# The first group of layer 2: B's parts between the softplus steps, six units from B's rows, the third softplus behind the first scan

## The chip, the core and the metric

The kernel runs on one core of a Trainium2 chip. The core has five engines, each with its own queue of instructions, which it works off in order: TensorE (PE, matrix products; its weight loads are shown as PEld), VectorE (DVE), ScalarE (ACT), GpSimd (POOL) and SyncE (SP), which here only issues transfers. Sixteen DMA engines move data between DRAM and the on-chip memories: SBUF, which every engine reads, and PSUM, which TensorE writes. The engines wait for one another by semaphores only. The metric is the device time of one launch in microseconds; the text gives all times in microseconds (us).

## What is computed

The reference passes an image of 64 x 64 positions and 96 channels through two layers. A layer normalises in groups, projects to 192 inner channels (and 192 more for a gate), runs a 3 x 3 convolution and a silu, and then four selective scans over the 4096 positions, in four orders. The scan is the costly part:

```
x_dbl = u @ x_proj;  dt = softplus(x_dbl[:6] @ dt_proj + bias);  B, C = x_dbl[6:22], x_dbl[22:38]
h[t] = h[t-1] * exp(dt[t] * A) + (dt[t] * u[t]) * B[t]      # for 192 channels x 16 states
y[t] = sum over the 16 states of h[t] * C[t];  y += u * D
```

The four y are put back in order and summed, normalised over channels, multiplied by the gate and projected to 96 channels, and the layer's input is added. The change is in layer 2's scans.

## The kernel before

Channels and states lie on the 128 partitions, positions along the free axis. Layer 2's scans (`scans`) run over 16 **groups** (one order and one chunk of 1024 positions each, `GROUPS`), and a group over 24 **units** (`units`): 3 blocks T of channels times 8 pairs m of states, in the order T = 0, 0, 1, 1, 2, 2 with even and odd m in turn. `PER` is 24. A unit j is made in these steps, one function each:

- `stage_a` (ACT): a = exp(dt * A), 128 x 1024.
- b, the input of the recurrence, in PSUM, in one of two ways. **By rows**: `stage_B` (PE) spreads two rows of B over the partitions with two bfloat16 products, and `stage_b` (DVE) multiplies them by du = dt * u. **By tokens**: `product` (ACT) multiplies du, transposed so that positions lie on the partitions (`duT`), by a column of B transposed (`BT`), sixteen such products for three units of odd m, and `stage_t` (PE) transposes eight pieces of the result `bT` back into PSUM; DVE has no part in it. Before, even units go by rows, odd ones by tokens.
- `stage_s` (DVE): the scan h = a * h + b. `stage_k` (ACT): the last column kept for the next chunk. `stage_c` (POOL): hc = h * C. `stage_r` (PE): sums over states; a block's first unit also brings in y.

What a group needs ahead of its units is its **prelude**: `project` (PE: pj = the rows of B, C and dt's input, in two halves h of 512 positions), `projected` (ACT: the copy xd), `first_part`, `less_part` and `next_part` (ACT and PE in turn: B split into three bfloat16 parts, B3, by subtracting what was rounded), `rows` (SP: C to DRAM), `tokens_B` and `tokens_B_out` (PE, ACT: BT), `delta` (softplus in three parts per block: `begin` on PE gives pd; `by_scalar`, four ACT instructions; `by_vector`, four DVE instructions, whose third is the last to read pd and writes sp = dt, whose fourth writes su = dt * u), `spread` (SP four transfers of sp to dt; for group 0 POOL issues four of su to du), `tokens_du` and `tokens_du_out` (PE, ACT: duT).

The order of all work is written out by hand: a queue of an engine holds what the program emits, in that order. The main loop runs over j and emits in iteration j, among others, `fetch_c` (SP: rows of C broadcast into cb), b's PE step of unit j+1, `stage_a(j+2)`, `stage_b(j)`, `stage_r(j-3)`, `stage_s(j)`, `stage_k(j-1)`, `stage_c(j-1)`, and then every step of the preludes whose slot is below j+1. Group k's slots count from the start of group k-1, so that group 1's prelude (`at[1]`) is emitted in group 0's units: `project` of half 0 in iteration 0, its copies and parts and the subtracting products in iterations 1 and 2, `project` of half 1 in iteration 2, and so on.

Group 0 has no group ahead of it. Its prelude is `first`, emitted whole before the loop: the six `start_y` of the layer's head on POOL (`later`, y = u * D), the projection, the ACT table load, the three softplus, then the split of B, the transposes of du and the sixteen products of the first three odd units (four on ACT, eight on DVE, four on POOL).

PSUM is shared by tags: a tile may be written only when the last reader of the tile before it under the same tag is done. Group 1's projections, its pd and its `tokens_B` all use tag "v", one after another; in `first`, pd of block 2 has "v", that of blocks 0 and 1 has "y2" and "b1". The products' b lie in "b0" and "b1". Tiles of a and h have three buffers each, so `stage_a(j)` waits for the scan of unit j-3, and the scan of unit j for `stage_c(j-3)`.

Of the kernel before, what the change touches and what calls it, by code (L numbers as in the profile page):

```python
# [9 lines left out]
F32 = mybir.dt.float32  # L10
# [14 lines left out]
TC = 1024  # L25
# [19 lines left out]
def two_ss2d_layers(  # L45
# [41 lines left out]
    def load_exp_ln():  # L87
        table("natural_log_exp_and_others")
# [17 lines left out]
    for h in range(2):  # L106
        t = const.tile([128, 128], F32, name=f"wide{h}")
# [49 lines left out]
    with tc.tile_pool(name="ld", bufs=8) as ld, tc.tile_pool(  # L157
        name="ldp", bufs=4, space=PSUM
# [81 lines left out]
    def decays(am):  # L240

        for a, e, D in am:
            for h, half in enumerate(HALF):
                tc.keep_in_program_order(
                    nc.scalar.activation(a[half, 0, 0:D], e[half, 0:D, :, h:NS:2], AF.Exp)
                )
            nc.vector.tensor_scalar_mul(a[:, 1, 0:D], a[:, 0, 0:D], -0.5)
            nc.vector.tensor_scalar_mul(a[:, 0, 0:D], a[:, 0, 0:D], -1.0)
        return [a for a, e, D in am]
# [15 lines left out]
    class Ordered:  # L265
# [7 lines left out]
    pe, act, dve, pool, sp = (  # L273
        Ordered(e) for e in (nc.tensor, nc.scalar, nc.vector, nc.gpsimd, nc.sync)
    )
# [516 lines left out]
    def scans(weights, pps, ready, later):  # L792
# [4 lines left out]
        xw, dwb, _ = weights  # L797
        class Ordered:
# [9 lines left out]
        pe, act, dve, pool, sp = (  # L808
            Ordered(e) for e in (nc.tensor, nc.scalar, nc.vector, nc.gpsimd, nc.sync)
        )  # L810
        with ExitStack() as sc:
# [42 lines left out]
            def prelude(k):  # L854
# [65 lines left out]
                def tokens_du(e):  # L920

                    ps = me["ps"] = me["tu", e] = spare(
                        f"tu{k}_{e}", "v" if k else ("y2", "v", "b0", "b1")[e]
                    )
                    for T in range(3):
                        pe.transpose(
                            ps[:, 128 * T : 128 * (T + 1)],
                            me["su", T][:, 128 * e : 128 * (e + 1)], ident,
                        )

                def tokens_du_out(e):
                    t = me["duT", e] = pre.tile(
                        [128, 2, 3, 64], F32, tag=f"duT{e}", name=f"duT{k}_{e}"
                    )
                    copy = act.copy if k or e < 2 else dve.tensor_copy
                    copy(t, me["tu", e][:, 0:384].rearrange("p (b h c) -> p h b c", h=2, c=64))


                def delta(T):
# [82 lines left out]

                steps = []
                if k == 0:
                    first(
                        project, projected, rows, delta, spread, tokens_B, tokens_B_out,
                        first_part, less_part, next_part, tokens_du, tokens_du_out,
                    )
                    return products(k)
                if (p, d) == (1, 0):  # L1030
                    steps += [(-17 + T, lambda T=T: turn(T)) for T in range(3)]

# [30 lines left out]
            def first(  # L1063
                project, projected, rows, delta, spread, tokens_B, tokens_B_out,
                first_part, less_part, next_part, tokens_du, tokens_du_out,
            ):
                parts = [delta(T) for T in range(3)]
                for start in later:
                    start()
                for h in range(2):  # L1070
                    project(h)
                for h in range(2):
                    projected(h)
                load_exp_ln()
                rows()
                for begin, by_scalar, by_vector in parts:
                    begin()
                tokens_B()
                for T, (begin, by_scalar, by_vector) in enumerate(parts):
                    by_scalar()  # L1080
                    if T == 1:
                        tokens_B_out()
                        am.extend(decays(weights[2]))
                    by_vector()
                    spread(T)
                    if T < 2:
                        fetch_c(0, T)
                stage_a(0)
                for h in range(2):
                    first_part(h)  # L1090
                for h in range(2):
                    less_part(h)
                for h in range(2):
                    next_part(0, h)
                for h in range(2):
                    less_part(h)
                for e in range(4):
                    tokens_du(e)
                for e in (0, 2, 1, 3):
                    tokens_du_out(e)  # L1100
                for h in range(2):
                    next_part(1, h)
                for e, engine in enumerate((act, dve, dve, pool)):
                    for h in range(2):
                        for n in range(2):
                            product(0, 0, e, h, n, engine)
                stage_B(0)
                stage_a(1)

            def products(k):  # L1110


                turns = (
                    (19, (4, 4, 4, 4)), (PER, (3, 1, 5, 1, 3, 3)), (PER + 6, (4, 2, 3, 1, 3, 3)),
                    (PER + 12, (2, 3, 3, 2, 3, 3)),
                )
                steps = []
                for i, (slot, counts) in enumerate(turns):
                    if (k, i) == (0, 0):
                        continue  # L1120
                    todo = [(e, h, n) for e in range(4) for h in range(2) for n in range(2)]
                    for s, count in enumerate(counts):
                        steps += [
                            (slot + s + 0.1, lambda i=i, at=at: product(k, i, *at))
                            for at in todo[:count]
                        ]
                        del todo[:count]
                return steps

            def product(k, i, e, h, n, engine=act):  # L1130


                me = state[k]
                if (h, n) == (0, 0):
                    me["bT", i, e] = mn.tile(
                        [128, 2, 3, 2, 64], F32, tag="bT", name=f"bT{k}_{i}{e}", bufs=7
                    )
                q = 2 * (2 * i + 1) + n
                (act.mul if engine is act else engine.tensor_scalar_mul)(
                    me["bT", i, e][:, h, :, n, :], me["duT", e][:, h],  # L1140
                    me["BT"][:, e + 4 * h, q : q + 1],
                )
# [55 lines left out]
            def fetch_c(k, m):  # L1198
                cb = state[k]["C", m] = mn.tile([128, TC], F32, tag="cb", name=f"cb{k}_{m}")
                for h, half in enumerate(HALF):  # L1200
                    q = 2 * m + h
                    sp.dma_start(
                        out=cb[half], in_=state[k]["C"][q : q + 1, :].to_broadcast(cb[half].shape)
                    )

            def stage_B(j):

                k, T, m = units[j]
                ps = live["b", j] = pps.tile([128, TC], F32, tag="b0", name=f"b{j}")
                for s in halves:  # L1210
                    pe.matmul(
                        ps[:, s], pick(GROUPS[k][1], m), state[k]["B3"][:, s], start=True, stop=True
                    )
# [14 lines left out]
            def stage_a(j):  # L1228
                k, T, m = units[j]
                p, d, c = GROUPS[k]  # L1230
                a = live["a", j] = mn.tile([128, TC], F32, tag="a", name=f"a{j}")
                act.activation(
                    a, state[k]["dt", T], AF.Exp, scale=am[p][:, 0, d, T, m : m + 1]
                )
# [60 lines left out]
            def unit(step, at):  # L1295
                if 0 <= at < N:
                    step(at)

            for j in range(N + LAG + 2):

                for ahead, odd in ((4, 0), (1, 1)):
                    k, i = divmod(j + ahead, PER)
                    if i % 6 == 0 and 0 <= k < len(GROUPS):
                        fetch_c(k, i // 3 + odd)
                unit(stage_B if j % 2 else stage_t, j + 1)
                while early and early[0][0] < j + 1:
                    early.pop(0)[1]()
                unit(stage_a, j + 2)
                if j % 2 == 0:
                    unit(stage_b, j)  # L1310
                unit(stage_r, j - LAG)
                unit(stage_s, j)
                unit(stage_k, j - 1)
                unit(stage_y, j - LAG - 1)
                unit(stage_c, j - 1)
                while steps and steps[0][0] < j + 1:
                    steps.pop(0)[2]()
# [594 lines left out]
```

## Time and profile before

| what | us |
|---|---|
| median of 3 runs (lowest, highest) | 1472.04 (1468.18, 1472.88) |
| the profiled execution, its own time | 1467.99 |
| its span | 1466.2 |
| busy in the span: DVE / ACT / POOL / PE | 1331.0 / 1222.5 / 1222.4 / 1195.6 |
| layer 2's last convolution product ends, its scans' first product starts (PE) | 245.5 |
| first scan of layer 2 starts (DVE) | 274.74 |

A timeline line gives the start (us from the span's start), the length, the engine, the instruction with output and inputs, how many of them are merged, and in brackets the engine's idle time before it with what seems to have ended it. A windows line gives a stretch, its length, the busy time and count of PE, PEld, DVE, ACT and POOL, then the share of TensorE's full clock that was granted (PEclk), the busy share of the DMA engines (which may pass 1 a little) and GB/s. All kernel work in `scans` carries one line number, L806, that of a helper, so tiles tell the steps apart: pj is `project`, tu `tokens_du`, b from B and selh `stage_B`, b from b and du `stage_b`, b from ident and bT `stage_t`, ys `stage_r`, sp, su and wl the softplus.

### The profile page before, as it was taken

The page shows a single profiled execution, that of the slowest core. Times are in us where ns is not written, and L with a number is a line of the kernel's source. Part 1 is how long each engine was busy: PE and PEld are TensorE (multiplying, and loading weights), DVE is VectorE, ACT ScalarE, POOL GpSimd, SP SyncE. Part 2 cuts the span into 40 slices and gives each one's busy share as a digit, 9 for nine tenths or more (in the row PEclk, how much of TensorE's full clock was granted, in tenths as well). Part 3 has the DMA queues.
Part 4 walks back from the last instruction along what each step waited for, and adds up shares of the span by engine and source line. Part 5 has one row for each costly group of instructions (what it writes and reads, how often), then busy time and mean ns, then how long its engine had stood idle before and what let it go on. Part 6 is the DMA issues. An engine that isn't in the chain of part 4 may idle for free.

```text
span 1466.2 us, 17295 instructions
## 1 busy us (share of the span) xinstructions
PE 1195.6 (82%) x5019; PEld 461.4 (31%) x5019; DVE 1331.0 (91%) x920; ACT 1222.5 (83%) x2517; POOL 1222.4 (83%) x684
## 2 busy tenths in 40 slices
PE   5865768688988797988898889788888888887887
PEld 2233223233333333333333333333333232322333
DVE  5958576689999999999999999999999999999996
ACT  4873557599899989999999999999898989897874
POOL 2735348588989898989898989898989898989895
PEclk8987879699999999999999999999999999999999
DMA  3251522526262626262626262626262626262635
GB/s 108 70 136 18 136 69 88 131 58 146 58 146 58 146 59 144 60 144 60 144 60 144 60 144 60 144 60 145 62 151 61 146 68 137 70 142 67 140 87 129
DMA packets 86261, 148.66 MB, mean 101 GB/s; under 512 B 34060, under 2 KB 37196, under 8 KB 86060
## 3 DMA queue, kind: packets, MB, share of 16 engines
q1 hardware_dynamic: 84188, 144.00, 41.0%
q0 software_dynamic: 864, 2.49, 0.7%
q10 hardware_dynamic: 1104, 0.98, 0.2%
q8 instruction: 40, 0.66, 0.2%
q14 instruction: 65, 0.53, 0.1%
HBM read 81.77 MB, written 12.17 MB: 64 GB/s over the span
## 4 chain that ended last, share of the span: by engine, by line
DVE 28%; issue 23%; POOL 10%; ACT 10%; PE 9%; DMA 7%; SPq 2%; DVEq 0%; POOLq 0%; ACTq 0%
DVE h L806 18%; DVE b L806 8%; POOL hc L806 7%; DMA cb<-C 4%; ACT a L806 3%; ACT bT L806 2%; PE ys L806 2%; SPq L806 2%; PE pj L806 1%; PE b L806 1%; POOL sp L806 1%; DMA xT<-xs 1%; DMA du<-su 1%; POOL ln L806 1%; PE cp L271 1%
## 5 line engine op out<-in xcount | busy, mean ns | idle before, releaser
L806 POOL TENSOR_TENSOR hc<-h,cb 128x1024 f32<-128x1024 f32 x384 | 902.3, 2368 | 91.4 <-DVE h L806 38.2
L806 DVE TENSOR_TENSOR_SCAN h<-a,carry,b 128x1024 f32<-128x1024 f32 x288 | 665.2, 2338 | 24.9 <-PE b L806 3.9
L806 ACT ACTIVATE a<-dt,am 128x1024 f32<-128x1024 f32 x384 | 438.1, 1141 | 63.3 <-DVE h L806 57.6
L806 PE MATMUL ys<-hc,fold 128*64 128x512 f32 x1536 | 429.5, 638 | 0.5 <-POOL hc L806 0.5
L806 ACT ACTIVATE bT<-duT,BT 128x192 f32<-128x192 f32 x1012 | 387.1, 445 | 3.4 <-PE b L806 1.3
L806 PE MATMUL b<-ident,bT 128*128 128x128 f32 x1536 | 220.0, 286 | 28.9 <-DVE h L806 21.0
L806 DVE TENSOR_TENSOR b<-b,du 128x1024 f32<-128x1024 f32 x192 | 232.0, 1208 | 4.9 <-PE b L806 4.9
L806 DVE TENSOR_TENSOR_SCAN h<-a,b 128x1024 f32<-128x1024 f32 x96 | 216.2, 2277 | 11.8 <-POOL hc L806 2.8
L806 PE MATMUL b<-B,selh 96*128 96x512 bf16 x384 | 116.2, 384 | 130.6 <-DVE h L806 129.7
L806 PEld LDWEIGHTS b<-ident,bT 128*128 128x128 f32 x1536 | 174.4, 145 | 151.3 <-DVE h L806 90.4
L806 PEld LDWEIGHTS ys<-hc,fold 128*64 128x64 f32 x1536 | 77.9, 138 | 141.7 <-issue 103.6
L806 PEld LDWEIGHTS <-selh 96*128 96x128 bf16 x384 | 25.8, 97 | 257.1 <-DVE h L806 201.0
L271 POOL TENSOR_TENSOR tap<-tap,tap 128x512 f32<-128x512 f32 x48 | 61.0, 1274 | 45.8 <-ACT tap L271 43.4
L806 PE MATMUL pj<-u,xw 64*124 64x512 f32 x192 | 91.5, 621 | 1.9 <-DVE w L806 1.2
L271 DVE SCALAR_TENSOR_TENSOR acc<-pad,v,acc 128x1052 f32<-128x1052 f32 (+1 forms) x64 | 75.3, 1182 | 2.1
L806 PE MATMUL ys<-y,ident 128*128 128x512 f32 (+1 forms) x120 | 59.6, 598 | 0.0
L806 ACT CAST B<-pj 96x512 bf16<-96x512 f32 (+2 forms) x96 | 54.9, 575 | 4.6 <-PE pj L806 4.5
L806 POOL TENSOR_TENSOR sp<-sp,ln 128x512 f32<-128x512 f32 x45 | 57.5, 1279 | 0.2
L806 POOL TENSOR_TENSOR ln<-ln,w 128x512 f32<-128x512 f32 x45 | 57.6, 1280 | 0.0
L806 POOL TENSOR_TENSOR su<-sp,u 128x512 f32<-128x512 f32 x45 | 57.4, 1276 | 0.0
L806 PE MATMUL pd<-xd,dwb 29*64 29x512 f32 x192 | 53.9, 634 | 0.0
L806 PEld LDWEIGHTS pj<-u,xw 64*124 64x124 f32 x192 | 33.1, 187 | 58.5 <-issue 44.1
(186 smaller groups left out, 1185.2 us busy)
## 6 DMA issues: line engine op xcount, KB each, us to landing
cb<-C SPq DMA_DIRECT2D x256, 256.0 KB
dt<-sp SPq DMA_DIRECT2D x192, 128.0 KB
du<-su SPq DMA_DIRECT2D x180, 128.0 KB
szd<-sz SPq DMA_DIRECT2D x24, 256.0 KB
szt<-szd SPq DMA_DIRECT2D x24, 256.0 KB
xT<-xs SPq DMA_DIRECT2D x8, 384.0 KB
xs<-xT SPq DMA_DIRECT2D x1, 1536.0 KB
xs<-xT SPq DMA_DIRECT2D x8, 192.0 KB
```

The source lines that it names most:

```text
L271: return lambda *args, **more: tc.keep_in_program_order(op(*args, **more))
L806: return lambda *args, **more: tc.keep_in_program_order(op(*args, **more))
```

## The change

In `first`, the ACT table load and `decays` (four small ACT exponentials, four DVE scalings) move ahead of the copies `projected`. The third softplus' `by_vector` and its `spread` leave `first` and become steps with slots `PER - 0.6` and `PER - 0.5` of group 0, that is -0.6 and -0.5 in the loop's count, emitted at the end of iteration 0, behind the first scan and ahead of group 1's first `project`. B's three parts are made between the softplus of the blocks, where before they came after all three. `tokens_du` and its copies move into iterations 1 and 2 (pieces 0 and 1, then 2 and 3), with all copies on ACT and PSUM tags "y2" and "y1"; within iteration 2 the order on PE is piece 2, group 1's `project` of half 1, piece 3. The sixteen products of units 1, 3 and 5 are dropped: units 0 to 5 all go by rows. The products of units 7, 9 and 11 are emitted at the end of iterations 2 to 5, four each. The last `start_y` on POOL moves to iteration 5.

```diff
 def tokens_du(e):
     ps = me["ps"] = me["tu", e] = spare(
-        f"tu{k}_{e}", "v" if k else ("y2", "v", "b0", "b1")[e]
+        f"tu{k}_{e}", "v" if k else ("y2", "y1")[e % 2]
     )
 ...
 def tokens_du_out(e):
 ...
-    copy = act.copy if k or e < 2 else dve.tensor_copy
-    copy(t, me["tu", e][:, 0:384].rearrange("p (b h c) -> p h b c", h=2, c=64))
+    act.copy(t, me["tu", e][:, 0:384].rearrange("p (b h c) -> p h b c", h=2, c=64))
 ...
 if k == 0:
-    first(
+    steps += first(
 ...
-    return products(k)
+    return steps + products(k)
 ...
 def first(...):
     parts = [delta(T) for T in range(3)]
-    for start in later:
+
+    def softplus(T):
+        parts[T][1]()
+        parts[T][2]()
+        spread(T)
+
+    for start in later[:-1]:
         start()
     for h in range(2):
         project(h)
+    load_exp_ln()
+    am.extend(decays(weights[2]))
     for h in range(2):
         projected(h)
-    load_exp_ln()
     rows()
     for begin, by_scalar, by_vector in parts:
         begin()
     tokens_B()
-    for T, (begin, by_scalar, by_vector) in enumerate(parts):
-        by_scalar()
-        if T == 1:
-            tokens_B_out()
-            am.extend(decays(weights[2]))
-        by_vector()
-        spread(T)
-        if T < 2:
-            fetch_c(0, T)
-    stage_a(0)
+    softplus(0)
+    fetch_c(0, 0)
     for h in range(2):
         first_part(h)
     for h in range(2):
         less_part(h)
+    tokens_B_out()
+    softplus(1)
+    fetch_c(0, 1)
     for h in range(2):
         next_part(0, h)
     for h in range(2):
         less_part(h)
-    for e in range(4):
-        tokens_du(e)
-    for e in (0, 2, 1, 3):
-        tokens_du_out(e)
     for h in range(2):
         next_part(1, h)
-    for e, engine in enumerate((act, dve, dve, pool)):
-        for h in range(2):
-            for n in range(2):
-                product(0, 0, e, h, n, engine)
     stage_B(0)
+    parts[2][1]()
+    stage_a(0)
     stage_a(1)
+    steps = [(PER - 0.6, parts[2][2]), (PER - 0.5, lambda: spread(2))]
+    for e in range(4):
+        o = PER + 1 + e // 2
+        steps += [
+            (o, lambda e=e: tokens_du(e)), (o + 0.1, lambda e=e: tokens_du_out(e)),
+        ]
+    return steps + [(PER + 5, later[-1])]
 ...
     if (k, i) == (0, 0):
         continue
+    if (k, i) == (0, 1):
+        slot, counts = PER + 2.3, (4, 4, 4, 4)
 ...
+def by_rows(j):
+    return j % 2 == 0 or j < 6
+
 def stage_B(j):
-    ps = live["b", j] = pps.tile([128, TC], F32, tag="b0", name=f"b{j}")
+    ps = live["b", j] = pps.tile([128, TC], F32, tag=f"b{j % 2}", name=f"b{j}")
 ...
-    unit(stage_B if j % 2 else stage_t, j + 1)
+    unit(stage_B if by_rows(j + 1) else stage_t, j + 1)
 ...
-    if j % 2 == 0:
+    if by_rows(j):
         unit(stage_b, j)
```

`product` also loses its choice of engine, since all products are now on ACT.

More of the change, by code (lines that the diff above doesn't have):

```diff
@@ L1128, in products, with product @@
                 return steps
-            def product(k, i, e, h, n, engine=act):
+            def product(k, i, e, h, n):
                 me = state[k]
@@ L1138, in product @@
                 q = 2 * (2 * i + 1) + n
-                (act.mul if engine is act else engine.tensor_scalar_mul)(
+                act.mul(
                     me["bT", i, e][:, h, :, n, :], me["duT", e][:, h],
```

## The prediction

> **What bounds the kernel now.** I read the page first, for the share of each engine and the slices in which DVE is not full; then the timeline from the end of layer 2's convolution to its steady scans; then narrow windows for the granted clock; last the landing times of du.
>
> ```profile
> PE 1195.6 (82%) x5019; PEld 461.4 (31%) x5019; DVE 1331.0 (91%) x920; ACT 1222.5 (83%) x2517; POOL 1222.4 (83%) x684
> DVE  5958576689999999999999999999999999999996
> PEclk8987879699999999999999999999999999999999
> L806 DVE TENSOR_TENSOR b<-b,du 128x1024 f32<-128x1024 f32 x192 | 232.0, 1208 | 4.9 <-PE b L806 4.9
> ```
>
> From the tenth slice on DVE is full: the scans bound the kernel, and what happens before is paid once. The eighth slice (256.6 to 293.2) has DVE at 6 tenths and the clock at 6 tenths: that is where this change lies.
>
> ```profile
> 264.25 1.15 ACT L806 ACTIVATE a<-dt,am 128x1024 f32<-128x1024 f32 x1 [4.18 <-DVE su L806]
> 269.99 1.02 DVE L806 COPY duT<-tu 128x384 f32<-128x384 f32 x2 [5.92 <-PE tu L806]
> 270.92 2.64 DVE L806 TENSOR_SCALAR bT<-duT,BT 128x192 f32<-128x192 f32 x8
> 274.48 2.84 PE L806 MATMUL pj<-u,xw 64*124 64x512 f32 x6
> 274.74 4.46 DVE L806 TENSOR_TENSOR_SCAN h<-a,b 128x1024 f32<-128x1024 f32 x2
> ...
> 282.56 5.48 PE L806 MATMUL pj<-u,xw 64*124 64x512 f32 x6
> 287.98 1.04 PE L806 MATMUL b<-B,selh 96*128 96x512 bf16 x2
> 288.81 1.92 PE L806 MATMUL ys<-y,ident 128*128 128x512 f32 x2
> 289.05 1.23 DVE L806 TENSOR_TENSOR b<-b,du 128x1024 f32<-128x1024 f32 x1 [3.99 <-PE b L806]
> 290.65 1.97 PE L806 MATMUL ys<-hc,fold 128*64 128x512 f32 x4
> 295.27 2.29 DVE L806 TENSOR_TENSOR_SCAN h<-a,b 128x1024 f32<-128x1024 f32 x1 [2.57 <-POOL hc L806]
> ```
>
> See two things. Ahead of the first scan (274.74) DVE idles 5.92: ACT stands 4.18 before a(0), and the split of B, the transposes and the products wait behind it. After it, DVE idles 3.99 for b of unit 4, which PE makes behind group 1's projection of half 1: the same six products took 2.84 at 274.48 and 5.48 at 282.56. The 2.57 at 295.27 is also PE's: `stage_t(5)` ends at 295.14, behind y's entry (1.92 + 1.97) and the subtractions.
>
> ```profile
> 274.00:276.00 2.00, 1.84 (x6) 0.93 (x6) 1.97 (x2) 1.48 (x4) 0.16 (x1) 1.00 1.08 287
> 284.00:286.00 2.00, 2.00 (x3) 0.65 (x2) 1.06 (x1) 0.76 (x2) 2.00 (x2) 0.50 0.00 0
> 286.00:288.00 2.00, 2.00 (x4) 0.35 (x3) 0.00 (x0) 0.00 (x0) 1.48 (x1) 0.50 0.00 0
> ```
>
> The clock is 1.00 in one and 0.50 in the other, and stays 0.50 though PE does nothing but the projection, all the time. In the rows it is 0.50 from 252.5 to 269.6 and from 279.8 to 293.5; it rises after stretches filled with the transposes of du and with the 128-row products of ys, not in the projection's 64-row ones.
>
> ```profile
> DMA to landing us min/median/max: 2.8/2.8/2.8
> DMA to landing us min/median/max: 5.3/5.7/6.1
> ```
>
> These are du's first transfer (issued 258.02) and its third and fourth: the last lands at 265.7. a(0) needs dt, issued by SP from 256.58, and am (258.4); so dt lands just before 264.25.
>
> **The change, up to the first scan.** The table load (1.28) now runs in ACT's 1.53 of waiting for pj; the four exponentials of `decays` (1.05 with gaps) stand ahead of the copies instead, which end 0.4 later (250.26), so pd of block 0 is ready at 251.05 and softplus 0 starts at 251.1 (251.21). Its ACT part takes 2.53, its DVE part 2.95: su at 256.8 (256.9). POOL, with five `start_y` of 2.88 instead of six, is free at 255.2, so du goes out at 257.1, 0.95 earlier. ACT then makes B's first part, BT, softplus 1 and the rest of B3 (to 259.6), and softplus 2's ACT part to 262.1, all inside the wait for dt. I let dt land at 264.0 and du's last at 264.8 (6.1 after issue): a(0) to 265.2, b(0) at 265.0, **first scan 266.3, 8.4 earlier**. Bounds: du 2.8 after issue, when a(0), 262.1 to 263.25, decides (scan at 263.4), and landing as now (scan at 267.1); I am nearer the second since the same transfers share the engines.
>
> The Trainium skill ("Trainium Kernel Development and Optimization", Key Constraints) says that DMAs issued from several engines run on the same 16 DMA engines and only save issue time; the windows show those engines at 1.01 of full from 258 to 260, and by that rule POOL's earlier issue buys nothing and the sum below would be 0.8 higher.
>
> **From the first scan on, PE decides.** Group 1's first projection needs tag "v", which block 2's pd holds until the moved `by_vector` has read it: four DVE instructions (2.95) from 268.5, the third done at 270.7. PE idles until then, so the clock is 0.50, and I take the slow price of every row, as the projection does not raise it. In PE's order: projection 270.8 to 276.3; B(2) (1.04) 277.3; piece 0 of du (duT's first two copies start 0.64 apart at the slow clock) 277.95; subtraction (0.55) 278.5; piece 1 279.15; ACT copies it (0.48) and makes the next part (0.58), done 280.4; subtraction 280.95; B(3) 282.0; piece 2 282.65; projection of half 1 (5.48) 288.1; piece 3 288.75; B(4) 289.8. DVE (b and scan 3.51 together, of which b 1.31): b(1) 271.4, scan 1 272.7 to 275.0; b(2) 277.3; b(3) 282.0; b(4) 289.8, **scan 4 at 291.1 (290.42 before)**. The lead is gone: before, the first projection ran warm in 2.84, and no du pieces lay between. Then y's entry 3.85 (1.92 + 1.97) to 293.65; the clock rises about there, as before; subtraction (0.4 fast) 294.05, ACT's next part 294.65, subtraction 295.1, B(5) (0.60) 295.6, scan 5 at 296.95 (295.27), scan 6 at 300.45.
>
> ACT, which stands for piece 3 until 289.0, then has the sixteen products of units 7 to 11 (1.45 per four) between a(5), a(6), a(7) (1.15 each), the copies and parts of half 1 and pd's first two steps: the last four end at 303.6, `stage_t(7)` at 304.0, **scan 7 at 304.05 (301.49)**.
>
> The same as a sum on DVE: first scan -8.4; `by_vector` moved behind it +2.95; b of units 1, 3 and 5, 3 x 1.31 = +3.9; idle time up to scan 7 from 7.4 (26.75 less seven scans at 2.2 and three b) to 2.35 + 1.1 + 4.2 + 2.25 + 1.4 = 11.3, +3.9; rounded **+2.6**. The dropped work (on DVE 2.64 and 1.02, POOL's four products at 753 ns, ACT's four at 445 ns) lay ahead of the old first scan and is in the 8.4. Moved issues: SP's four dt transfers of block 2 wait until 270.7 and hold back the cb of units 6 on, not needed before 303; POOL's four du issues (2.1) go ahead of hc(0), now at 273.9, which PE reads at 289.8. The last `start_y` (2.85) fits between hc(4), ending 295.8, and hc(5), from 299.2: nothing, or 2.85 if it meets no gap. Behind scan 7 the shift stays: POOL runs without a break of over 0.4 from 303.9 to 345, and ACT is busy 37.9 of 40 from 300 to 340.
>
> So 1467.99 + 2.6 = 1470.6 against the profiled execution, which lies 4.05 under the median of the runs: **1474.6** on their scale, as are all times below.
>
> **The rule against it.** The Trainium skill ("TensorE: Matmul & The Clock Gate", Part 1: The HAM clock gate) says that about 3.4 us of sustained busy time opens the clock; by it the projection would open it itself and the sum would be -2 to -4. The windows at 284 to 288 show otherwise: busy throughout, 0.50.
>
> **Rivals.** (1) The clock rises when the projection ends, at 276.3, through du's pieces: B(2) 276.9, b(3) 280.6, projection of half 1 281.3 to 284.15, B(4) 285.3, scan 5 at 291.9, products to 298.8, scan 7 at 299.3: -2.2, 1469.8. For it: at 266 to 269.6 subtractions and du's transposes raised it; against: those were eight transposes close together, here three at a time. (2) The clock is up from 270.8: projection to 273.65, no wait for B(2), scan 4 at 283.6, scan 7 at 296.3: **-5.2, 1466.8**, the only way to a clear gain; it decides if PE warms before the projection, but PE does only short subtractions and two B from 254 to 262 and then nothing for 9. (3) The clock stays low until about 303: subtractions, B(5), B(6), pd and the entry of block 1 at the slow price, scan 7 2.5 later: +5.1, 1477.1. For it: the rise needs a full stretch, and only the 3.85 of y's entry is one. (4) `start_y` is not hidden: +5.45, 1477.5. That the scan does not start earlier at all would need du after 273; nothing speaks for that.
>
> **How the numbers follow.** A measurement here tells 0.3% (4.4) from no change: 1467.6 and 1476.5. Forecast 0.50, of which 0.08 beyond +4.4 (late landing, scatter of the runs, 1468.18 to 1472.88); (1) 0.16, of which 0.03 faster than 0.3%; (2) 0.13; (3) 0.15; (4) 0.06. Faster 0.16, same 0.55, slower 0.29. The forecast's own range by the landing bounds (-0.3 to +3.4): 1471.7 to 1475.4. The range reaches from just under (2) to past (3) and (4) with the scatter: 1466 to 1479.
>
> **What would show it.** First scan near 266; projection of half 0 right behind the third `by_vector`, 5.5 long at clock 0.50; DVE idle before b(2) and, longest, before b(4); ACT idle before duT's last copy; scan 7 near 304. Wrong if either projection takes 2.8, if the first scan is before 264 or after 267, or if POOL or ACT has slack after unit 7 that takes the shift back.

## The result and the profile after

The changed kernel took 1474.87 us (median of 20 runs, 1469.31 to 1492.33) against 1473.51 for the kernel before (20 runs, 1468.17 to 1479.73): ratio 1.0011, 95% interval 0.9991 to 1.0031, that is between 1.3 faster and 4.6 slower. A difference from zero is not shown. The longest of its 20 runs, 1492.33, lies over 1.5% above the fastest and is left out of the ratio as a slow run. The profiled execution took 1477.95, with a span of 1476.2; the pair of profiles differs by 10.0, which the medians do not show.

From the page of the changed kernel: the busy time of each engine, two rows of slices and one group (busy time and mean ns of one, then idle time before them).

```profile
PE 1205.6 (82%) x5001; PEld 464.1 (31%) x5001; DVE 1332.0 (90%) x913; ACT 1223.2 (83%) x2515; POOL 1220.1 (83%) x680
DVE  5958677688999999999999999999999999899996
PEclk8987888589999999999999999999989999899999
L806 DVE TENSOR_TENSOR b<-b,du 128x1024 f32<-128x1024 f32 x195 | 235.7, 1209 | 14.9 <-PE b L806 12.0
```

DVE does 3 more b (195 for 192) and waits 14.9 for them instead of 4.9. In the slices, DVE gains a tenth in the fifth, which lies ahead of the change, and in the seventh, and loses one in the tenth, and the granted clock of the eighth falls from 6 tenths to 5. Next is DVE in the timeline of the changed kernel; the bracket is the idle time before.

```profile
263.11 1.23 DVE L806 TENSOR_TENSOR b<-b,du 128x1024 f32<-128x1024 f32 x1 [2.98 <-DMA du<-su]
264.45 2.29 DVE L806 TENSOR_TENSOR_SCAN h<-a,b 128x1024 f32<-128x1024 f32 x1
...
268.08 0.69 DVE L806 SCALAR_TENSOR_TENSOR sp<-pd,wl 128x512 f32<-128x512 f32 x1
...
275.31 1.23 DVE L806 TENSOR_TENSOR b<-b,du 128x1024 f32<-128x1024 f32 x1 [2.28 <-PE b L806]
...
287.23 1.23 DVE L806 TENSOR_TENSOR b<-b,du 128x1024 f32<-128x1024 f32 x1 [4.08 <-PE b L806]
288.59 2.29 DVE L806 TENSOR_TENSOR_SCAN h<-a,b 128x1024 f32<-128x1024 f32 x1
292.26 1.23 DVE L806 TENSOR_TENSOR b<-b,du 128x1024 f32<-128x1024 f32 x1 [1.38 <-PE b L806]
...
303.00 2.29 DVE L806 TENSOR_TENSOR_SCAN h<-a,b 128x1024 f32<-128x1024 f32 x1 [3.47 <-PE b L806]
```

The first scan is at 264.45 instead of 274.74, 10.29 earlier (0.9 of that comes from ahead of the stage, whose first product starts at 244.57 instead of 245.47). At scan 4 (288.59 for 290.42) 1.83 of that is left, and scan 7 (303.00 for 301.49) is 1.51 late. PE's timeline shows what DVE waited for:

```profile
268.82 5.48 PE L806 MATMUL pj<-u,xw 64*124 64x512 f32 x6 [7.98 <-DVE sp L806]
274.23 1.03 PE L806 MATMUL b<-B,selh 96*128 96x512 bf16 x2
...
280.03 5.48 PE L806 MATMUL pj<-u,xw 64*124 64x512 f32 x6
285.44 0.90 PE L806 MATMUL tu<-ident,su 128*128 128x128 f32 x3
286.13 1.06 PE L806 MATMUL b<-B,selh 96*128 96x512 bf16 x2
286.98 1.74 PE L806 MATMUL ys<-y,ident 128*128 128x512 f32 x2
...
295.77 1.97 PE L806 MATMUL pd<-xd,dwb 29*64 29x512 f32 x4
297.67 2.08 PE L806 MATMUL ys<-y,ident 128*128 128x512 f32 x2
299.68 1.98 PE L806 MATMUL ys<-hc,fold 128*64 128x512 f32 x4
301.58 1.31 PE L806 MATMUL b<-ident,bT 128*128 128x128 f32 x8
```

The projection of group 1 begins as soon as the third softplus on DVE has read pd (268.82), takes 5.48 in both halves, and b of units 2 and 4 stand behind it. The granted clock, the column that follows the five engines' busy times, goes with the 5.48 (before, the same six products took 2.84 at 1.00):

```profile
282.00:286.00 4.00, 4.00 (x8) 1.44 (x7) 1.15 (x1) 0.00 (x0) 2.34 (x1) 0.50 0.00 0
...
288.00:290.00 2.00, 1.74 (x6) 0.32 (x5) 1.87 (x2) 2.00 (x5) 0.00 (x0) 0.89 0.00 0
...
296.00:302.00 6.00, 6.00 (x12) 1.28 (x11) 3.40 (x2) 5.97 (x15) 2.79 (x3) 0.50 0.41 110
```

It is 0.50 through the projection, rises at 288.4 during y's entry, and is 0.50 again from 295.3 to 302.1, where the pd, the y entry of block 1 and `stage_t(7)` stand.

Behind scan 7 the two profiles part further. The shift is 1.5 up to unit 14, then 4.6 at unit 16, where the clock of the changed kernel fell to 0.50 once more (326.0 to 332.8). Whether that stretch belongs to the change is open: three variants of the changed kernel below have one of 6.8 or more between 318 and 337 too, the kernel before has none there. The shift is 2.2 at unit 192 and 10.2 at unit 360, with further low stretches at 1261 to 1271, 1312 to 1319 and 1340 to 1347. Low stretches come in every profile of these kernels, and not at the same places. Nothing in the change acts at those later places, and the medians do not show the 10: a single pair of profiles is good for the group that the change touches, not for the total.

### The profile page after: what moved, and what is told of

Read it like the earlier page. It is cut to its first block, busy times and chain, and to the rows that moved or that the text cites. A ratio compares the mean times of both kernels' runs of the same rounds, so it can differ in the third digit from the quotient of the medians.

```text
span 1476.2 us, 17242 instructions
## 1 busy us (share of the span) xinstructions
PE 1205.6 (82%) x5001; PEld 464.1 (31%) x5001; DVE 1332.0 (90%) x913; ACT 1223.2 (83%) x2515; POOL 1220.1 (83%) x680
## 4 chain that ended last, share of the span: by engine, by line
DVE 30%; issue 22%; PE 14%; ACT 10%; POOL 6%; DMA 4%; SPq 2%; DVEq 0%; POOLq 0%; ACTq 0%
DVE h L806 19%; DVE b L806 9%; POOL hc L806 4%; PE ys L806 4%; ACT a L806 3%; PE pj L806 3%; SPq L806 2%; DMA cb<-C 2%; PE b L806 2%; ACT bT L806 2%; PE pd L806 1%; DMA xT<-xs 1%; DMA dt<-sp 1%; PE cp L271 1%; POOL sp L806 1%
## 5 line engine op out<-in xcount | busy, mean ns | idle before, releaser
L806 DVE TENSOR_TENSOR b<-b,du 128x1024 f32<-128x1024 f32 x195 | 235.7, 1209 | 14.9 <-PE b L806 12.0
L806 PE MATMUL b<-ident,bT 128*128 128x128 f32 x1512 | 215.0, 286 | 26.4 <-DVE h L806 21.3
L806 PE MATMUL b<-B,selh 96*128 96x512 bf16 x390 | 120.6, 392 | 134.6 <-DVE h L806 134.3
L806 PE MATMUL pj<-u,xw 64*124 64x512 f32 x192 | 97.5, 655 | 10.0 <-DVE sp L806 8.0
```

Of the source, the lines that this page charges most:

```text
L806: return lambda *args, **more: tc.keep_in_program_order(op(*args, **more))
```

## The experiments

Eleven variants were made. To take out small shifts of layer 1 and of layer 2's head, all scan times in this section are counted from the start of the first product of `project` (245.47 in the profile of before, 244.57 in that of after). The columns are starts of scans in the one profiled execution of each; the last column is the ratio to the kernel before, measured in the same set of runs.

| kernel | scan 0 | scan 4 | scan 7 | scan 12 | scan 16 | ratio, 95% interval |
|---|---|---|---|---|---|---|
| before | 29.27 | 44.94 | 56.02 | 72.17 | 85.43 | 1 |
| after | 19.88 | 44.02 | 58.43 | 74.58 | 90.90 | 1.0011 [0.9991, 1.0031] |
| third softplus ahead | 21.26 | 41.10 | 53.89 | 70.39 | 85.23 | 0.9994 [0.9967, 1.0021] |
| 128-row products ahead | 19.82 | 42.01 | 55.16 | 71.31 | 87.66 | 1.0002 [0.9976, 1.0029] |
| 64-row products ahead | 20.16 | 44.77 | 58.02 | 74.17 | 90.96 | one run, 1483.15 |
| du's pieces ahead | 20.11 | 44.18 | 58.01 | 74.17 | 87.63 | 0.9981 [0.9958, 1.0003] |
| order of `first` alone | 26.66 | 44.49 | 54.47 | 70.62 | 83.88 | 0.9974 [0.9947, 1.0001] |
| order of `first`, half 1 later | 26.66 | 40.41 | 50.06 | 66.91 | 89.48 | 1.0036 [1.0013, 1.0059] |
| after, half 1 later | 19.93 | 39.88 | 50.59 | 68.27 | 89.27 | one run, 1470.52 |
| third ahead, half 1 later | 21.12 | 35.91 | 47.20 | 64.04 | 86.26 | 0.9985 [0.9958, 1.0012] |
| the same, and v free in time | 21.12 | 36.08 | 47.08 | 65.85 | 79.11 | 0.9915 [0.9884, 0.9946] |
| after, half 1 later, v free in time | 20.08 | 40.04 | 50.64 | 69.40 | 82.65 | 0.9956 [0.9936, 0.9975] |
| order of `first`, half 1 later, v free | 27.20 | 40.95 | 51.40 | 70.17 | 85.00 | 0.9988 [0.9959, 1.0017] |

**The third softplus.** It goes back ahead of the first scan; all else stays as in the changed kernel.

```diff
 parts[2][1]()
+parts[2][2]()
+spread(2)
 stage_a(0)
 stage_a(1)
-steps = [(PER - 0.6, parts[2][2]), (PER - 0.5, lambda: spread(2))]
+steps = []
```

> All changes stay but one: the third softplus' four DVE instructions and its transfers are emitted again before the loop, ahead of b(0). Times from the first product of `project` (before: first scan at 29.3, scan 4 at 45.0, scan 7 at 56.0; after: 19.9, 44.0, 58.4). Theory (PE's queue behind the moved softplus eats the lead): DVE does them in its wait for du, b(0) starts at most 2 later, but group 1's first projection starts 4.6 earlier; scan 4 at 39 to 40, scan 7 at 53 to 54, total 4 to 5 below the changed kernel. Rival (the lead went into DVE's own added work, three b and the moved softplus): only what fits into DVE's wait comes back, 1 to 2 at scan 4 and scan 7.

The first scan is 1.38 later than in the changed kernel, scan 7 4.54 earlier (53.89). So the place of the third softplus costs the changed kernel 4.5 at scan 7 and buys 1.4 at scan 0. That is what the first theory gave for scan 7 (53 to 54); scan 4 at 41.10 is 1.1 later than its 39 to 40, and the time is that of before, where 4 to 5 below the changed kernel was expected: there remains one long wait. From this variant's timeline, ACT, PE and DVE in turn:

```profile
276.76 1.15 ACT L806 ACTIVATE a<-dt,am 128x1024 f32<-128x1024 f32 x1 [2.22 <-DMA dt<-sp]
```

```profile
278.52 5.48 PE L806 MATMUL pj<-u,xw 64*124 64x512 f32 x6 [1.21 <-ACT B L806]
283.94 1.03 PE L806 MATMUL b<-B,selh 96*128 96x512 bf16 x2
```

```profile
285.01 1.23 DVE L806 TENSOR_TENSOR b<-b,du 128x1024 f32<-128x1024 f32 x1 [5.28 <-PE b L806]
```

ACT stands at a(4) for dt of block 2, so the last part of half 0 is late, the second projection waits for it and b(4) stands behind 5.48 of cold products. The wait moved from half 0 to half 1.

**The clock.** Five products that nobody reads (ten instructions on PE) are put between B(1) and the projection, once with 128 rows and once with 64, so that PE is busy in both. ROWS stands for 128 or 64.

```diff
+def warm():
+    ps = spare("warm", "y2")
+    for _ in range(5):
+        pe.matmul(ps, ident[0:ROWS], chunk(u[0], 0)[0:ROWS], start=True, stop=True)
+
+steps += [(PER - 0.55, warm)]
```

> The changed kernel with five products of 128 rows, whose result nobody reads, put on PE between B(1) and group 1's first projection, where PE stands idle for 8 us. Theory (the clock at half makes the two projections 5.5 long): the clock is at 1.00 when the projection starts, it takes 2.8, b(2) waits under 0.5 and b(4) under 1.5; scan 4 at 39 to 40.5, scan 7 at 53 to 55, total 3 to 5 below the changed kernel. Rival (the order of the queue alone decides, not the clock): both stay within 1 of the changed kernel's 44.0 and 58.4, or get later because the extra products stand in the queue.

> As warm128, with 64 rows of the same operands instead of 128 in the five products that nobody reads. If the rise of the clock needs products over all rows, as the projection's behaviour suggests: the clock stays at 0.50 through them, the first projection takes 5.5, scan 1 to 7 within 1 of the changed kernel. If sustained busy time alone raises it: as warm128, the first projection takes 2.8 and scan 2 is at 29.6 instead of 32.1.

PE and the granted clock, 128 rows (windows, then PE's timeline):

```profile
262.00:266.00 4.00, 4.00 (x6) 1.50 (x5) 1.74 (x2) 3.06 (x4) 1.47 (x3) 0.53 0.98 232
268.00:272.00 4.00, 2.27 (x6) 1.02 (x6) 3.79 (x6) 0.97 (x1) 0.92 (x2) 1.00 1.05 218
```

```profile
261.64 6.50 PE L806 MATMUL warm<-u,ident 128*128 128x512 f32 x10
269.87 2.85 PE L806 MATMUL pj<-u,xw 64*124 64x512 f32 x6 [1.73 <-DVE sp L806]
...
279.12 5.48 PE L806 MATMUL pj<-u,xw 64*124 64x512 f32 x6 [0.46 <-ACT B L806]
```

and 64 rows:

```profile
261.00:266.00 5.00, 5.00 (x7) 1.83 (x6) 1.89 (x3) 3.95 (x5) 2.04 (x4) 0.50 1.06 226
266.00:271.00 5.00, 5.00 (x7) 1.94 (x6) 4.90 (x6) 0.47 (x1) 0.01 (x1) 0.50 1.06 217
```

```profile
261.70 8.90 PE L806 MATMUL warm<-u,ident 64*128 64x512 f32 x10
270.40 4.47 PE L806 MATMUL pj<-u,xw 64*124 64x512 f32 x5
```

(The list for 64 rows breaks off at 274; the six products of that projection take 5.32.) With 128 rows the clock rises, the first projection takes 2.85 instead of 5.48 and scan 7 comes 3.27 earlier than in the changed kernel. With 64 rows PE is fully busy for 10 us and the clock stays at 0.50. So the forecast's choice, that the projection does not raise its own clock, held, and the gain from a warm first projection is 3.3 in this pair of profiles. The theory had more (scan 4 at 39 to 40.5, scan 7 at 53 to 55; measured 42.01 and 55.16). Half 1 was cold again at 279.12: the clock fell before it. The time of this variant equals that of before, and its later scans carry clock lows of their own (2.2 later than before at scan 16), so the saving at scan 7 did not reach the total in a form that these runs can tell.

**du's pieces, ahead of the second projection.** The forecast had scan 7 set by ACT's products, which wait for the last piece of du. Here all four pieces go ahead of `project` of half 1.

```diff
-    o = PER + 1 + e // 2
+    o, out = ((PER + 1, PER + 1.1), (PER + 1.5, PER + 2.05))[e // 2]
     steps += [
-        (o, lambda e=e: tokens_du(e)), (o + 0.1, lambda e=e: tokens_du_out(e)),
+        (o, lambda e=e: tokens_du(e)), (out, lambda e=e: tokens_du_out(e)),
     ]
```

> The changed kernel with the last two pieces of du transposed ahead of B(3) and of the projection of half 1, their copies right behind the next part of half 0's last step. Theory: ACT no longer stands 5.8 for piece 3 and makes the products of units 7 to 11 earlier; scan 4 within 0.5 of 44.0, scan 7 2 earlier if the products set it. Rival: scan 7 is set by PE (pd of block 0 and the entry of block 1 ahead of the transposes of unit 7), and nothing changes by more than 0.5 at either.

Scan 7 moved by 0.42 only. By itself this decides little, since the products moved hardly more: their end comes 0.46 earlier, counted from the first product of `project`. The timeline decides. In this variant PE (columns as above) and ACT end ahead of scan 7 as follows:

```profile
298.81 2.07 PE L806 MATMUL ys<-y,ident 128*128 128x512 f32 x2
300.81 1.98 PE L806 MATMUL ys<-hc,fold 128*64 128x512 f32 x4
302.72 1.95 PE L806 MATMUL b<-ident,bT 128*128 128x128 f32 x8
```

```profile
300.49 1.48 ACT L806 ACTIVATE bT<-duT,BT 128x192 f32<-128x192 f32 x4
```

The last products are done at 301.97 and PE comes to them at 302.72: PE decides. It is the same in the changed kernel itself, where they end at 300.24 and `stage_t(7)` starts at 301.58, right behind the y entry at clock 0.50.

**The reordering alone.** From the kernel before: table load and `decays` first, B's parts between the softplus; all three softplus ahead of the first scan, then du's transposes and the sixteen products of units 1, 3 and 5, as before.

```diff
     project(h)
+load_exp_ln()
+am.extend(decays(weights[2]))
 for h in range(2):
     projected(h)
-load_exp_ln()
 ...
+softplus(0)
+fetch_c(0, 0)
 ...
+tokens_B_out()
+softplus(1)
+fetch_c(0, 1)
 ...
+softplus(2)
+stage_a(0)
 ...
```

> The kernel before with only the first part of the change: table load and decays ahead of the copies, B's parts made between the softplus of the blocks; tokens for units 1, 3 and 5, all softplus and all six start_y before the loop, as before. Theory: the transposes of du, which waited for B's parts, start some 3 earlier; they still raise the clock ahead of the projection, so the first scan is at 25.5 to 26.5 and the lead of 3 holds to scan 7 (53 to 53.5); total 3 below the kernel before. Rival (the stretch is set by the transfers or by PE anyway): under 1 at scan 7.

The first scan is 2.61 earlier, scan 4 0.45 earlier, scan 7 1.55 earlier, where the theory had 53 to 53.5 and measured is 54.47; the time is 3.8 lower by the ratio, with an interval that just reaches no change. The lead went in the same place as in the changed kernel: the clock did not rise, and the first projection took 5.48 (before: 2.84). It did not rise although ten of du's twelve transposes stand together and PE has hardly a gap from there to the projection; what made the difference to the kernel before is open. From its timeline:

```profile
264.39 2.40 PE L806 MATMUL tu<-ident,su 128*128 128x128 f32 x10 [4.24 <-DVE su L806]
...
270.99 5.48 PE L806 MATMUL pj<-u,xw 64*124 64x512 f32 x6
```

```profile
287.58 1.23 DVE L806 TENSOR_TENSOR b<-b,du 128x1024 f32<-128x1024 f32 x1 [3.99 <-PE b L806]
```

So of the changed kernel's 9.4 at scan 0 (19.88 for 29.27), 2.6 is the reordering, and the other 6.8 the dropped products, the moved transposes, softplus and `start_y`; the moved softplus is the smaller part, as with the third softplus put back ahead the first scan is only 1.38 later.

**The projection's place in PE's queue.** If b(4) waits because `project` of half 1 stands ahead of it, then moving that half behind B(4) removes the wait. Group 1's second half goes one unit later, and its three softplus with it.

```diff
-1: ((0, 1, 1.2, 2), (2, 3, 3.2, 4), 3, 4.1, 4.3),
+1: ((0, 1, 1.2, 2), (3, 4, 4.2, 5), 4, 5.1, 5.3),
 ...
-o, slots = 3 * T, (5, 5, 5, 6, 6, 6, 7, 8, 8.5 + T // 2, 9 + T // 2)
+o, slots = 3 * T, (6, 6, 6, 7, 7, 7, 8, 9, 9.5 + T // 2, 10 + T // 2)
```

It was made on the version with the third softplus ahead, on the changed kernel itself, and on the reordering alone:

> As third_early (third softplus before the loop), and group 1's projection of half 1, with all that hangs on it, one iteration later: PE makes B(4) and the entry of block 0 ahead of it, and group 1's softplus is one slot later. Theory (what DVE waits for is what stands ahead of B in PE's order): b(4) no longer waits, scan 4 at 35.5 to 37 (third_early 41.1); the wait moves to b(5) and is smaller: scan 5 at 41 to 44.5 (46.8), scan 7 at 50 to 52 (53.9); total 2 to 4 below third_early. Rival (the projection's 5.5 are only moved): scan 5 at 46 to 47, scan 7 within 0.7 of 53.9.

> The changed kernel with nothing but the later projection of half 1. Theory: DVE's wait of 4 before b(4) is the projection's place in PE's queue; scan 4 at 39 to 40.5 (44.0), scan 5 at 45.5 to 49 (49.1), scan 7 at 54 to 58 (58.4). Rival (b(4) waits for its du or for the scan before): scan 4 stays within 0.5 of 44.0.

> As reorder_only (units 1, 3 and 5 by tokens), and group 1's projection of half 1 with what hangs on it one iteration later. Theory: scan 4 at 40.5 to 41.5 (44.5), scan 5 at 46 to 49.5 (48.3), as `stage_t(5)` now stands behind the projection, scan 7 at 52.5 to 55 (54.5); total 0 to 2 below reorder_only. Rival: same as there, or later by what the entry of block 0 puts ahead of the projection, 1 to 2.

Scan 4 comes 5.2, 4.1 and 4.1 earlier than without the move, scan 7 6.7, 7.8 and 4.4. In the changed kernel with the move, DVE takes up b(4) and scan 4 without a wait:

```profile
283.50 1.21 DVE L806 TENSOR_TENSOR b<-b,du 128x1024 f32<-128x1024 f32 x1
284.84 2.29 DVE L806 TENSOR_TENSOR_SCAN h<-a,b 128x1024 f32<-128x1024 f32 x1
```

The second projection now stands behind y's entry, during which the clock has risen, and takes 2.83 or 2.84 in all three; scan 7 (47.20, 50.59 and 50.06) comes earlier than each theory gave, which had 50 to 52, 54 to 58 and 52.5 to 55. The cause of the 4.08 before b(4) is shown: the place of the projection in the queue. How much of it a warm projection in the old place would have left was not run. But the total did not follow, against the theories: the third of these is slower than before (0.36%), the first not measurably faster. The lead is lost between scans 12 and 16, which in the first lie 22.2 apart (13.3 before). The timeline of the first of the three, around there:

```profile
320.68 4.68 PE L806 MATMUL pj<-u,xw 64*124 64x512 f32 x6 [2.51 <-DVE w L806]
...
325.29 1.97 PE L806 MATMUL b<-ident,bT 128*128 128x128 f32 x8
...
327.37 2.29 DVE L806 TENSOR_TENSOR_SCAN h<-a,b 128x1024 f32<-128x1024 f32 x1 [6.83 <-PE b L806]
```

Group 2's first projection needs tag "v", which pd of block 2 of group 1 holds until a DVE instruction of its softplus (w) has read it. That softplus is now one unit later, the projection's slot is not; PE stands 2.51, and b behind it makes DVE wait 6.83.

**v free in time.** The same three, with group 1's first softplus one unit later as above, the second half a unit, and the third at its old place.

```diff
-o, slots = 3 * T, (6, 6, 6, 7, 7, 7, 8, 9, 9.5 + T // 2, 10 + T // 2)
+o, slots = 3 * T, (
+    (6, 6, 6, 7, 7, 7, 8, 8.5, 8.9, 10),
+    (6, 6, 6, 6, 7, 7, 7, 8, 8.5, 9),
+    (5, 5, 5, 6, 6, 6, 7, 8, 9.5, 10),
+)[T]
```

> The third softplus ahead of the first scan, group 1's second projection one unit later, and of its three softplus the first one unit later, the second half a unit, the third at its old place, so that tag v is read free before group 2's first projection as in the kernel before. If what lost the lead between units 12 and 16 was that projection's wait for v (2.51, and b of a unit behind it, 6.83 on DVE), scan 7 comes at 46 to 48 after the first projection product, unit 12 at 63 to 65, unit 16 at 76.5 to 80 (86.3 with the late third softplus alone, 85.4 before), and the time is 5 to 9 below the kernel before in the same call. Rival: POOL and ACT hold no more than 3.3 per unit and the lead runs out anyway, unit 16 at 83 or later, the time within 3 of before.

> The same slots on the version that only reorders the first group (products for units 1, 3 and 5 kept, third softplus ahead of the first scan). The theory of the wait for v: scan 7 at 49.5 to 51, unit 12 at 66 to 68, unit 16 at 79 to 83 (89.5 without the new slots), the time 3 to 6 below before. The rival: unit 16 at 85 or later, the time within 3 of before.

> The changed kernel with its own place for the third softplus (behind the first scan), and only the slots of group 1's prelude moved (second projection and first softplus one unit later, second softplus half a unit, third at its old place). If the order behind the first scan is what cost the changed kernel its lead, and the third softplus' place costs 3.5 on top (scan 7 50.6 against 47.1 with it ahead of the first scan), unit 7 comes at 50 to 51.5, unit 16 at 82 to 84, and the time is 2 to 5 below the kernel before. Rival: the 3.5 is taken up by waits behind unit 7 that the version with the third softplus ahead has and this one has not; then unit 16 comes at 79 to 80.5 and the time is as that one's, 1458 to 1465 (0.988 to 0.995 of before).

With the third softplus ahead: scan 7 at 47.08, scan 16 at 79.11, **1461.51 us against 1472.91, ratio 0.9915 [0.9884, 0.9946]**. The gain is beyond the 5 to 9 of the theory, scan 12 (65.85) a little later than its 63 to 65. It is faster than the kernel before by an interval clear of 1, from six runs; the changed kernel did not run beside it, but has 1.0011 to the same kernel before. PE's timeline, first the projection of half 1 of group 1, then the first of group 2:

```profile
282.10 2.84 PE L806 MATMUL pj<-u,xw 64*124 64x512 f32 x6
284.87 0.61 PE L806 MATMUL b<-B,selh 96*128 96x512 bf16 x2
```

```profile
317.51 2.81 PE L806 MATMUL pj<-u,xw 64*124 64x512 f32 x6 [1.07 <-DVE w L806]
```

PE waits 1.07 instead of 2.51, and the projection takes 2.81 instead of 4.68. The second difference is the clock, which was low in the earlier variant from 62.1 to 72.3 and 75.7 to 82.5 and here, between scans 8 and 16, only from 65.0 to 68.4; how much of the 7.2 at scan 16 is the tag and how much the clock was not separated.

With the third softplus at its place behind the first scan (the changed kernel otherwise), scan 7 is at 50.64 and scan 16 at 82.65, both inside what the first theory gave, and the time is 6.1 lower than before (0.9956), 1 more than its 2 to 5. The place of the third softplus costs 3.5 at scans 7 and 16, and of the two times the difference is 6.0 (0.0041 of 1473); each of the two ratios has 3 to 5 either way, so the difference has about 5 and is only just clear of none.

On the reordering alone the new slots give scan 16 at 85.00, where 79 to 83 was expected: the miss began earlier, as scan 12 was 3.3 later than with the old slots. The time is that of before. There the lead is lost on the way between scans 7 and 16, partly in two low stretches of the clock (67.6 to 71.0 and 77.9 to 81.3); which of the waits there comes first was not traced further.

The totals of the two best variants fall by more than their scans show in the profile (6.3 and 2.8 at scan 16, for 11.4 and 6.1). Single profiles carry clock lows at differing places, so the rest is not explained by anything shown here.

## Why the prediction was right or wrong

The forecast of no measurable change, 1474.6, met 1474.87; the two agree more closely than the runs of one kernel among themselves, and that closeness is luck. The 1474.6 is 2.6 on top of the 1472.04 of three runs; over 20 runs the kernel before took 1473.51, and the change is +1.4 with an interval from -1.3 to +4.6. The 2.6 itself is what the forecast's walk gives at scan 7 (304.05 for 301.49); its sum's terms, -8.4, +2.95, +3.9 and +3.9, come to 2.35. By its steps:

- **First scan 266.3, within 263.4 to 267.1.** 264.45: inside, 1.85 early. The term that was mis-sized is the transfers' landing. POOL issued du at 256.75 (forecast 257.1), and b(0) could start at 263.11, 6.36 after the first issue; the forecast took du's end at 264.8. Before it was 258.02 and 265.7, 7.7. Half of the 1.85 is the earlier start of the whole stage (244.57 for 245.47): counted from there, the first scan is 0.95 early, and du went out 0.37 earlier than before and landed 1.7 earlier. Why the transfers took less is open. The Trainium skill ("Trainium Kernel Development and Optimization", Key Constraints) says that transfers issued from several engines share the same 16 DMA engines and that this saves issue time only; it does not say that an earlier issue buys nothing, as the forecast took it, and here the landing did come earlier, though the DMA engines stood at 1.05 of full from 262 to 266.
- **Projection of half 0 right behind the third `by_vector`, 5.48 at clock 0.50.** Right: 268.82 to 274.3, PE idle 7.98 before it. The experiments show both halves of this: with 128-row products ahead it takes 2.85, and 64-row products do not help.
- **DVE idles 2.35, 1.1, 4.2, 2.25 and 1.4, together 11.3.** Measured 2.28, 0.56, 4.08, 1.38 and 3.47, together 11.77. All five are right in place; the first and the third are close in size, the second and the fourth half a us and 0.9 shorter, the fifth 2.1 longer. The cause given for the longest, that b(4) stands behind the second projection, was shown by moving that projection.
- **y's entry cold (3.85), the clock rising at its end.** The term was too dear by 1: the clock rose at 288.42, 1.4 after the entry began, and the entry took 2.8 (1.74 and 1.08). Scan 5 came 5.0 after scan 4, not 5.85.
- **Scan 7 at 304.05, set by ACT's products.** 303.00. The size (+2.6; +1.51 in the span, +2.4 counted from the first projection product) was nearly right, the reason was not. The products were done at 300.24; `stage_t(7)` came at 301.58, behind pd and the y entry of block 1 on PE, at clock 0.50. That is the mechanism of rival 3, in a second low stretch (295.3 to 302.1) instead of one that lasts. The earlier first scan (1.85) and the longer wait here (3.47 for 1.4) nearly cancelled, so the nearness of the size is in part luck.
- **`start_y` hidden between hc(4) and hc(5).** Right: 293.36 to 296.2, hc(5) at 296.17, 0.3 after scan 5's end.
- **The shift stays behind scan 7.** The medians (+1.4, from -1.3 to +4.6) fit +1.5 to +2.6, but are too wide to show it. In the one pair of profiles it grew to 10.2, through clock lows that the forecast had not in its sum: on the profile's scale it said 1470.6, and that execution took 1477.95.
- **Rival 2, the clear gain of 5.2 with a warm first projection.** Its condition was made for the first projection only (128-row products), and scan 7 came 0.9 before that of before, not 5.2: the second projection was cold again, which the rival had as warm. What a clock that stays up would have given was not run.

## What to carry to other kernels

A lead won ahead of a stage is worth what is left of it at the first tile that waits for an in-order queue; look for the next long instruction group that stands ahead of it there, and for the buffer that this group waits for, before you shorten anything. Here the 9.4 won at the first scan were more than lost by scan 7, 11.8 in all: some 6.8 went into what DVE itself had to do more (the moved softplus, 2.76, and three b at 1.34), and 4.8 into longer waits for PE (11.77 for 6.95), where two projections stayed in front of b. Moving one of them by a unit, and the softplus that frees its successor's buffer back, brought the changed kernel from 1.0011 to 0.9956 of the kernel before. When one step is shifted in a hand-written order, follow its buffer to the next user: a shift of one unit showed its price some dozen units later.

## What the runs showed of the hardware

What raises TensorE's clock is not busy time alone. The page "TensorE: Matmul & The Clock Gate" of the Trainium skill (Part 1: The HAM clock gate) has the clock full after some 3.4 us of sustained busy time. Here, in one run, 64-row float32 products kept PE at 5.00 of 5.00 us in two windows running, and the granted clock stayed 0.50; ten 128-row products in the same place took it from 0.50 to 1.00, at 265.74, 4.1 after the first began. It did not last: it was 0.50 again from 272.57, at the end of a projection of 64-row products. Nor did 128 rows always do it: with the reordering alone, ten transposes of 128 rows together left it at 0.50. What else counts is not shown.

The clock changes on a grid. In each of the thirteen profiles, from 250 to 360, the time from one change to the next is a whole multiple of 3.41 (before: 252.53, 269.60, 279.84 and 293.49, that is 5, 3 and 4 times), and the grid does not lie at the same place in every execution. So the 4.1 above is no threshold, and neither is the 1.4 after which the clock rose in y's entry. That entry took 2.8 in the changed kernel and 3.8 in the variant with 128-row products, with the same instructions.

The scatter of the runs goes with the granted clock: over the 20 runs of the changed kernel, the correlation of time and mean clock is -0.86 (-0.76 without the longest). For example, 1470.2 had a mean clock of 0.938 and 1485.16 one of 0.919, though 1469.31 had 0.933. A few microseconds in one group of units therefore need many runs to be seen in the total.
